# Where the slots of a mixture-of-experts layer go in a planned instruction stream: one chain, one piece a step, and the residual's store on another queue

## The chip, the cores and the metric

The kernel runs on one core of a Trainium2 chip. The metric is the device time of one execution in microseconds (us); the time of a kernel is the median of its runs. The engines are TensorE (PE in the profile; its weight loads are the row PEld), VectorE (DVE), ScalarE (ACT), GpSimd (POOL) and SyncE (SP, which only issues transfers here). Each of them works off its own list of instructions in order, and waits on semaphores for the others. Transfers between DRAM and the on-chip memory are issued by an engine's instruction and carried out by 16 DMA engines.

## The reference

The input is `x`, four sequences of 512 rows of 256 numbers, and a context of four times 1024 rows of 128. Two decoder layers follow each other, each made of residual blocks of the form `x = x + f(layernorm(x))`: a linear attention over landmarks, a causal attention that also reads the context (16 heads), a quantised linear layer; then a causal attention with hyperbolic distances, a block of two multi-head attentions with an MLP each (256 to 1024 to 256), and at last a mixture of experts. The change touches the order of work in the second block of the first layer and in the last two blocks of the second layer. The last one is:

```python
gate_scores = jax.nn.softmax(x @ Wg + bg, axis=-1)          # 8 experts
topk_scores, topk_idx = jax.lax.top_k(gate_scores, 2)
topk_scores = topk_scores / (jnp.sum(topk_scores, axis=-1, keepdims=True) + 1e-08)
combine_w = jnp.einsum('bsk,bske->bse', topk_scores, jax.nn.one_hot(topk_idx, 8))
for e in range(8):
    h = jax.nn.gelu(x @ W1[e] + b1[e])                      # 256 -> 1024
    y = h @ W2[e] + b2[e]                                   # 1024 -> 256
    output = output + y * combine_w[..., e:e + 1]
```

Here `x` is normalised; the block returns the unnormalised `x` plus `output`.

## The kernel before

**Slots.** The experts are not run on all rows. Each of the 2048 rows is copied (`scatter`, L1664: an indirect DMA, L1667, for 128 rows and one of their two choices, so eight for a batch) to its place in a table `rows` in DRAM, sorted by expert. The table is then worked off in `NSLOT` = 39 slots of 128 rows, each of one expert. For a slot the kernel fetches the rows (`fetch_z`, tile `zs`, 130 KB) and all weights of the slot's expert (`fetch_w`, tile `we`, 2052 KB, four buffers), both issued by SP (L1787 to L1807). Its work on the engines has three kinds of pieces. `turn` (L1809) transposes the rows on TensorE and makes on VectorE the row's target `to` (L1818) and its weight `wts` (L1820, L1821). `hidden` (L1823), in two halves, is the first layer: 16 matmuls (L1830) and 4 GELUs on ScalarE (L1832) a half. `output` (L1834) is the second layer, 16 matmuls (L1837, two for each of the program's eight calls), one multiplication on VectorE into `ys` (L1839) and one indirect DMA issued by POOL (L1840) that *adds* the 128 rows to the table `sums` in DRAM. `ys` has three buffers, `to` and `wts` four.

**What `sums` begins with.** Once a batch has passed the gate, `biases2` (L1683) puts the experts' second biases into `x`, and after its second half the batch's `x` is written to `sums` (L1688, L1689), issued by POOL. The slots' additions come on top of that. At the end `Slots.end` (L1876) copies `sums` to the output, two batches by SP and two by ScalarE.

**Early and late slots.** Which expert a slot belongs to depends on the data. After three of the four batches the first 16 slots (`NEARLY`) that are certainly full are known: `count_early` and `table_early` run as pieces of batch 2's gate, and `go` marks that the slots may begin. The other 23 are known after batch 3: `count_late` (L1771, whose `steps` issues 16 memsets on POOL, L1720) and `table_late` (L1776) are pieces of batch 3's gate, after `rank` (L1643) and ahead of `biases` (L1672, whose transposes are L1679), and `rest` (L1433 in the block's MLP) then adds their work.

**Who sets the order.** The program is written out by hand. `Stream` (L310 to L591) is a planner that runs while the program is built. A stream has *jobs*, here groups of four attention heads, and each job has first-pass tiles (`d_tile`, L381, scores and row maxima) and second-pass tiles (`a_tile`, L421, scores again, exponentials, values). A step `t` holds at most one first-pass tile (`d_at`) and one second-pass tile (`a_at`). All other work, such as norms, MLPs, gates, the slots, is cut into pieces and put into *chains*. A piece is a list of earliest step, due step, gap to the piece before, cost and function. A positive cost is time on TensorE, a negative one time on VectorE, zero is free. `chain` (L333) appends a chain. In each step `run` (L530) first lays the pieces that are due (`force`, L373), then the tiles, then calls `fill` (L357), which goes on laying the piece with the nearest due step while `room` (L369) allows it:

```python
return not cost or self.spent[k] == 0.0 or self.spent[k] + abs(cost) / 2 <= rates[k]
```

So the first piece of a step always goes, and further ones only up to the step's rate for TensorE (`rates[0]`) or VectorE (`rates[1]`). While there are first-pass tiles, the rate is worked out from the due steps; when there are none left it is fixed, 3.0 for both (L358). That is the case at the end of two streams: `l0_xattn` (the second block of layer 0) and `l1_xattn` (the double attention, whose end is also the gate and the slots).

**The slots in the planner.** When `go` has run and the attention is over, `tail` (L1293) closes the attention's pools and chains what `Slots.begin` (L1844) returns. It fetches rows of 16 slots and weights of three at once, and then, slot by slot (`round`, L1861): fetch of the slot after the next two (cost 0), two halves of `hidden` of the next slot (2.0 each), `turn` of the one after (0.5), `output` of this one (3.4). `rest` (L1433) makes a second chain of the rounds of the late slots. All these pieces have a due step far away, so they go behind the gate's pieces. `leave` (L1436) builds a batch's gate chain from the list that `gate` returns (L1691), and inserts the counting pieces by position from its end.

**The end of the other stream.** In `l0_xattn` each batch's preparation for the next attention (`front.batch`, 54 pieces, chained at L719 with `spill=True`) may be left over when the stream ends; its last pieces are given to `l1_attn` (L1014), whose `pump` (L1055) lays one at a time between its own units. That stage loads `qk` (L1069) from the DRAM tile `qk_d`, which these pieces fill (stores at L992), and multiplies it from L1092 on.

Of the kernel before, what the change touches and what calls it, by code (L numbers as in the profile page):

```python
# [20 lines left out]
P = 128  # L21
# [19 lines left out]
def decoder_kernel(ctx: ExitStack, tc: tile.TileContext, a: dict, out: bass.AP):  # L41
# [3 lines left out]
    def ts(i, n=P):  # L45
        return slice(i * n, (i + 1) * n)
# [263 lines left out]
    class Stream:  # L310
# [22 lines left out]
        def chain(self, items, spill=False):  # L333
            items = [[*i] for i in items]
            for i, j in zip(items[-2::-1], items[:0:-1]):
                i[1] = min(i[1], j[1])
            self.chains.append(SimpleNamespace(items=deque(items), at=-99, spill=spill))

        def lay(self, c):
            cost, fn = c.items.popleft()[3:]  # L340
# [14 lines left out]
            return rates  # L355

        def fill(self):  # L357
            rates = self.rates() if self.t in self.d_at else [3.0, 3.0]  # L358
            while True:
                ready = [  # L360
                    c for c in self.chains
                    if max(c.items[0][0], c.at + c.items[0][2]) <= self.t
                    and self.room(rates, c.items[0][3])
                ]
                if not ready:
                    return
                self.lay(min(ready, key=lambda c: c.items[0][1]))
# [871 lines left out]
    def l1_xattn(cn_d, moe, early):  # L1239
        with early.stack as st:  # L1240
# [52 lines left out]
            def tail():  # L1293
                if slots.ready:
                    inner.close()
                    s.chain([(s.t + 4, 10**6, 0, c, f) for c, f in slots.begin(st)])
                return slots.ready

            def block(k, b):
# [97 lines left out]
                def mlp():  # L1397
                    def li1(t):
                        ps = ring()
                        for g in range(4):  # L1400
                            PE.matmul(ps[:, 0:C], e.yT[:, g, ts(t)], w["li1"][:, g, :], start=g == 0, stop=g == 3)
                        add_to(e.xo[:, t, :], ps[:, 0:C])

                    def mid():
                        e.nT = one.tile([P, 2, T], F32, name="nT5", tag="nT5")
                        G.tensor_add(x1, x1, e.xo)
                        G.tensor_add(x1, x1, mid_bc(bl3, NT))

                    def li2(f):
                        if f == 0:  # L1410
                            e.h = one.tile([P, 8, T], F32, name="hT5", tag="hT5")
                        ps = ring()
                        for c in range(2):
                            PE.matmul(ps, w["li2"][:, c, ts(f)], e.nT[:, c, :], start=c == 0, stop=c == 1)
                        if f % 2:
                            S.activation(e.h[:, f, :], ps, AF.Identity, bias=pv[:, 12 + f : 13 + f])
                        else:
                            V.tensor_scalar_add(e.h[:, f, :], ps, pv[:, 12 + f : 13 + f])

                    def gelu():  # L1420
                        S.activation(e.h, e.h, AF.Gelu)
                        S.preload_act_table_set("natural_log_exp_and_others")
                        if k:
                            e.kept = one.tile([P, NT, C], F32, name="kept", tag="xo")
                            nc.sync.dma_start(e.kept, kept[b])

                    def li3(t):
                        ps = ring()
                        for f in range(8):
                            PE.matmul(ps[:, 0:C], e.h[:, f, ts(t)], w["li3"][:, f, :], start=f == 0, stop=f == 7)  # L1430
                        add_to(x1[:, t, :], ps[:, 0:C])

                    def rest():  # L1433
                        s.chain([(s.t, 10**6, 0, c, f) for c, f in slots.rest()])

                    def leave():  # L1436
                        if k:
                            G.tensor_add(x1, x1, e.kept)
                            g = gate(
                                moe, b, SimpleNamespace(), gs,  # L1440
                                lambda: one.tile([P, 2, T], F32, name="hT6", tag="hT6"), ring,
                            )
                            more = {
                                B - 2: [(1, 1.0, slots.count_early), (1, 1.0, slots.table_early)],
                                B - 1: [(1, 1.0, slots.count_late), (1, 1.0, slots.table_late)],
                            }.get(b, [])
                            g[-7:-7] = more
                            if more:
                                g[-3:-3] = [(0, 0.0, rest if b == B - 1 else slots.go)]
                            s.chain([(s.t, s.t + 2 + int(0.7 * i), gap, c, f) for i, (gap, c, f) in enumerate(g)])  # L1450
                        back.add(b)
                        if not k and b == B - 1:
                            ffn_weights("a2", ws[1])

                    t0 = s.t
                    work = [(True, 1.7, lambda: li1(0))] + [(False, 1.7, lambda t=t: li1(t)) for t in range(1, 4)]
                    work += [(1, -1.2, p) for p in ln_pieces(e.xo, z3)]
                    work += [(0, 0.0, mid), (True, 0.5, lambda: flip(e.z3, 0, [(e.nT, 8)]))]
                    work += [(False, 0.5, lambda: flip(e.z3, 1, [(e.nT, 8)]))]
                    work += [(f == 0, 1.7, lambda f=f: li2(f)) for f in range(8)]  # L1460
                    work += [(True, 0.0, gelu)]
                    work += [(t == 0, 3.4, lambda t=t: li3(t)) for t in range(4)]
                    work += [(False, 0.0, leave)]


                    lag, pace = {(0, 0): (1, 1.0), (0, B - 1): (3, 1.1), (1, B - 2): (2, 0.65)}.get((k, b), (3, 1.0))
                    s.chain([
                        (t0, t0 + (1 if i < 4 else lag + int(pace * (i - (i > 8)))), gap, c, f)
                        for i, (gap, c, f) in enumerate(work)
                    ])  # L1470
# [100 lines left out]
    def gate(m, b, e, gs, hT, bank):  # L1571
# [111 lines left out]
        def biases2(h):  # L1683
            ps = bank()
            for t in range(2):
                PE.matmul(ps[:, ts(t, C)], e.cT[:, ts(2 * h + t)], m.b2, start=True, stop=True)
            V.tensor_add(xb[:, ts(h, 2), :], ps.rearrange("p (t c) -> p t c", c=C), xb[:, ts(h, 2), :])
            if h:  # L1688
                G.dma_start(m.sums[ts(b, T), :].rearrange("(t p) c -> p t c", p=P), xb)  # L1689

        return (  # L1691
            [(2 if i == 0 else 1, -1.2, p) for i, p in enumerate(ln_pieces(xb, z))]
# [1 line left out]
            + [(1, -1.5, choose), (1, -1.2, choose2), (1, -1.2, choose3), (1, 0.5, rank)]  # L1694
            + [(t == 0, 0.0, lambda t=t: scatter(t)) for t in range(NT)]
            + [(1, 0.7, biases), (1, 0.9, lambda: biases2(0)), (0, 0.9, lambda: biases2(1))]
        )


# [312 lines left out]
```

## Time and profile before

| | us |
|---|---|
| median of 3 runs (lowest, highest) | 3477.65 (3476.08, 3499.53) |
| the profiled execution's own time | 3483.41 |
| its span | 3481.7 |
| TensorE, matmuls | 3066.6 busy, 88%, 19095 instructions |
| VectorE | 2092.8 busy, 60%, 5138 |
| ScalarE | 1902.4 busy, 55%, 3845 |
| GpSimd | 815.4 busy, 23%, 679 |
| granted TensorE clock, mean | 0.915 of full |
| DMA | 174.52 MB, mean 50 GB/s |

The span runs from the first to the last recorded instruction of one execution; the execution's own time is 1.7 us longer. Slices are 1/40 of the span, 87 us each. A group row gives the line, the engine and the operation, the tiles written and read, the number of instructions, then busy time and the mean of one, then the engine's idle time ahead of them and what ended most of it. In a row of windows each pair of brackets belongs to an engine (busy time and number of instructions, in the order TensorE matmuls, weight loads, VectorE, ScalarE, GpSimd), followed by the granted clock, the busy share of the DMA engines and GB/s. A timeline row has the start, the duration, the engine and the line; what stands in brackets at its end is the idle time before it and its releaser.

Three transfers matter here, with the median time from issue to landing: `we<-in_we`, 39 of 2052 KB, 9.1 us; `zs<-rows`, 39 of 130 KB, 8.8 us; `sums<-x`, four of 512 KB, 4.5 us.

### The profile page before, as it was taken

To read this page: it belongs to the slowest core of one execution; us is meant where nothing else is said; L and a number is where in the kernel's file an instruction comes from. 1 tells how busy PE (TensorE), PEld (TensorE's weight loads), DVE (VectorE), ACT (ScalarE), POOL (GpSimd) and SP (SyncE) were. 2 spreads that over 40 slices of the span, in tenths; PEclk is the share of its full clock that TensorE was granted. 3 is DMA by queue.
4 is the path that set the end of the run, shared out by engine and by line. 5 is a ranking of instruction groups with operands and counts; after the bars stand their busy time and mean duration, and the time that the engine had idled before them with its cause. 6 is when DMAs were issued, how large, how long until landed. Compare 5 with 4: busy or idle time off the path is not lost. (4 is left out here: it accounts for less than half of the span.)

```text
span 3481.7 us, 50606 instructions
## 1 busy us (share of the span) xinstructions
PE 3066.6 (88%) x19095; PEld 1497.5 (43%) x19095; DVE 2092.8 (60%) x5138; ACT 1902.4 (55%) x3845; POOL 815.4 (23%) x679
## 2 busy tenths in 40 slices
PE   6689999999998666677899999999999998987997
PEld 3433333334334344344434444433333333447896
DVE  4576676777765687876676565665746646433111
ACT  2225555454554764779588676556663664542221
POOL 1010112122022745668212121100101201122111
PEclk9889999999999567777799999999998999999998
DMA  9100000010001100120000000000000000045896
GB/s 287 55 28 7 1 7 3 6 31 4 10 19 42 49 6 32 37 86 7 25 1 1 1 4 16 7 1 31 13 1 5 21 1 13 13 172 172 288 310 190
DMA packets 78405, 174.52 MB, mean 50 GB/s; under 512 B 5640, under 2 KB 61200, under 8 KB 72976
## 3 DMA queue, kind: packets, MB, share of 16 engines
q1 hardware_dynamic: 68304, 155.47, 12.9%
q0 software_dynamic: 7728, 11.47, 1.5%
q10 hardware_dynamic: 2128, 4.34, 0.3%
q8 instruction: 150, 2.46, 0.3%
q14 instruction: 95, 0.78, 0.1%
HBM read 125.46 MB, written 47.90 MB: 50 GB/s over the span
## 5 line engine op out<-in xcount | busy, mean ns | idle before, releaser
L426 ACT ACTIVATE pt<-ps_s 128x512 f32<-128x512 f32 (+2 forms) x1536 | 792.1, 569 | 744.8 <-PE ps_s L425 649.6
L390 PE MATMUL ps_s<-kT,qT 32*128 32x512 f32 (+3 forms) x3072 | 923.0, 623 | 45.7 <-ACT pt L426 27.9
L402 DVE TENSOR_REDUCE mx<-ps_s 128x1 f32<-128x512 f32 x768 | 489.7, 684 | 221.7 <-PE ps_s L390 123.2
L390 PEld LDWEIGHTS ps_s<-kT,qT 32*128 32x128 f32 x3072 | 309.8, 186 | 338.8 <-issue 96.9
L394 DVE TENSOR_REDUCE mx<-ps_s 128x1 f32<-128x512 f32 x512 | 328.5, 685 | 193.4 <-PE ps_s L390 190.1
L425 PE MATMUL ps_s<-qa,kT 32*128 32x512 f32 (+3 forms) x1536 | 440.5, 588 | 4.5 <-ACT pt L426 3.1
L425 PE MATMUL ps_s<-qT,kT 32*128 32x512 f32 x1536 | 418.6, 638 | 0.0
L406 ACT ACTIVATE ps_s<-ps_s,mx 128x512 f32<-128x512 f32 x512 | 340.8, 670 | 27.5 <-DVE mx L394 27.0
L1832 ACT ACTIVATE hid<-ps_s,we 128x128 f32<-128x128 f32 x312 | 88.9, 368 | 236.4 <-issue 146.1
L1109 POOL TENSOR_TENSOR s<-s,mh 128x1280 f32<-128x1280 f32 x64 | 186.7, 2942 | 81.9 <-ACT mh L1108 64.1
L398 DVE CUSTOM_DVE_ANT_0 junk<-ps_s,dmask 128x256 f32<-128x256 f32 (+3 forms) x256 | 125.6, 491 | 92.0 <-PE ps_s L425 40.3
L1830 PE MATMUL ps_s<-zsT,we 128*128 128x128 f32 x1248 | 153.6, 283 | 26.6 <-DMA we<-in_we 14.8
L167 POOL TENSOR_TENSOR ln_r<-ln_ve,mhalf 128x4 f32<-128x4 f32 x40 | 40.8, 1020 | 532.5 <-DVE ln_ve L162 468.7
L1830 PEld LDWEIGHTS ps_s<-zsT,we 128*128 128x128 f32 x1248 | 150.9, 199 | 32.4 <-issue 17.1
L425 PEld LDWEIGHTS ps_s<-qa,kT 32*128 32x128 f32 x1536 | 143.3, 184 | 47.3 <-DVE mx L402 23.9
L1092 PE MATMUL ps_s<-qk 32*128 32x256 f32 (+3 forms) x512 | 103.2, 609 | 67.2 <-DVE mh L1097 56.5
L418 PE MATMUL ps_s<-qm,all 3*128 3x512 bf16 x768 | 156.9, 388 | 5.9 <-ACT ps_s L406 3.1
L1124 POOL TENSOR_TENSOR s<-s 128x1280 f32<-128x1280 f32 x64 | 147.6, 2337 | 12.3 <-ACT s L1120 12.3
L1151 DVE COPY pt<-ps_s 128x512 f32<-128x512 f32 x160 | 108.4, 688 | 62.0 <-PE ps_s L1149 62.0
L1149 PE MATMUL ps_s<-ident,s 128*128 128x128 f32 x640 | 130.5, 341 | 16.5 <-ACT s L1143 15.3
L1837 PE MATMUL ps_s<-we,hid 128*128 128x256 f32 x624 | 141.7, 381 | 0.0
L1097 DVE TENSOR_SCALAR_CACHE_REDUCE mh<-ps_s 128x512 f32<-128x512 f32 (+3 forms) x256 | 108.5, 487 | 51.7 <-PE ps_s L1096 27.4
(435 smaller groups left out, 5155.1 us busy)
## 6 DMA issues: line engine op xcount, KB each, us to landing
we<-in_we SPq DMA_DIRECT2D x39, 2052.0 KB, 9.1
rows<-zero SPq DMA_DIRECT2D x8, 2080.0 KB, 19.1
qk_d<-qkT SPq DMA_DIRECT2D x32, 256.0 KB, 2.5
qk<-qk_d SPq DMA_DIRECT2D x8, 1024.0 KB, 6.2
zs<-rows SPq DMA_DIRECT2D x39, 130.0 KB, 8.8
li<-in_a_li SPq DMA_DIRECT2D x4, 1024.0 KB, 5.5
v_d<-vp SPq DMA_DIRECT2D x16, 143.5 KB, 1.8
v<-v_d SPq DMA_DIRECT2D x4, 574.0 KB, 6.8
```

The costliest lines, as they stand in the source:

```text
L390: PE.matmul(ps[:, 0:n], u.qT[r, ts(qt)], u.kT[r, hf * 512 : hf * 512 + n], start=True, stop=True)
L394: V.tensor_reduce(m, ps[:, 0:n], AX.X, ALU.max, negate=True)
L402: V.tensor_reduce(m, ps[:, 0:n], AX.X, ALU.max)
L406: S.activation(ps, ps, AF.Exp, bias=m, accum_out=sm)
L418: PE.matmul(ps, self.ones[r, :], u.qm[r, :], start=True, stop=False)
L425: PE.matmul(ps[:, c0:], u.kT[r, ts(kt)], (u.qa if u.first_row else u.qT)[r, c0:], start=u.first_row, stop=True)
L426: S.activation(u.pt[:, j, c0:], ps[:, c0:], AF.Exp, scale=u.scale)
L1109: G.tensor_add(s, s, m)
L1124: G.tensor_mul(s, s, s)
L1149: PE.transpose(ps[:, ts(j)], u.s[h // 2][:, h % 2, c0 : c0 + P], ident)
L1830: PE.matmul(ps[:, ts(f)], u.w[:, k : k + P], u.zT[:, c, :], start=c == 0, stop=c == 1)
L1837: PE.matmul(ps[:, 0:C], u.h[:, f, :], u.w[:, 2048 + f * C : 2048 + f * C + C], start=f == 0, stop=f == 7)
```

## The change

There are four edits.

1. `fill` uses a TensorE rate of 1.0 instead of 3.0 in steps that have no first-pass tile. With `room` as above, a step then gets one TensorE piece beside pieces of cost zero, unless a second one is cheap enough (0.5 after 0.5 or 0.7). VectorE's rate stays 3.0.
2. `tail` keeps the early slots' chain in `slots.chain`, and `rest` appends the late slots' pieces to it (and lists the chain again if it has run empty) instead of making a chain of their own.
3. The store of a batch's `x` into `sums` is no longer part of `biases2(1)` and no longer issued by POOL; it is a piece of its own, the gate's last one, a step later or more, of cost zero, issued by ScalarE.
4. Since the gate's list is one longer, the two positions at which the counting pieces and `go` or `rest` are inserted move by one, so that they stay at the same places.

```diff
             self.chains.append(SimpleNamespace(items=deque(items), at=-99, spill=spill))
+            return self.chains[-1]
...
         def fill(self):
-            rates = self.rates() if self.t in self.d_at else [3.0, 3.0]
+
+            rates = self.rates() if self.t in self.d_at else [1.0, 3.0]
...
                     inner.close()
-                    s.chain([(s.t + 4, 10**6, 0, c, f) for c, f in slots.begin(st)])
+                    slots.chain = s.chain([(s.t + 4, 10**6, 0, c, f) for c, f in slots.begin(st)])
...
                     def rest():
-                        s.chain([(s.t, 10**6, 0, c, f) for c, f in slots.rest()])
+                        c = slots.chain
+                        if not c.items:
+                            s.chains.append(c)
+                        c.items.extend([s.t, 10**6, 0, cost, f] for cost, f in slots.rest())
...
-                            g[-7:-7] = more
+                            g[-8:-8] = more
                             if more:
-                                g[-3:-3] = [(0, 0.0, rest if b == B - 1 else slots.go)]
+                                g[-4:-4] = [(0, 0.0, rest if b == B - 1 else slots.go)]
...
             V.tensor_add(xb[:, ts(h, 2), :], ps.rearrange("p (t c) -> p t c", c=C), xb[:, ts(h, 2), :])
-            if h:
-                G.dma_start(m.sums[ts(b, T), :].rearrange("(t p) c -> p t c", p=P), xb)
+
+        def store():
+            nc.scalar.dma_start(m.sums[ts(b, T), :].rearrange("(t p) c -> p t c", p=P), xb)
...
             + [(1, 0.7, biases), (1, 0.9, lambda: biases2(0)), (0, 0.9, lambda: biases2(1))]
+            + [(1, 0.0, store)]
```

## The prediction

> **What bounds the kernel now.** I read the page's slices first: TensorE is busy nearly throughout, but in the last ten slices the DMA row climbs from 0 to 9 while VectorE, ScalarE and GpSimd fall to 1. So the end is a stage of its own, the mixture-of-experts slots. Then the chain that ended last:
>
> ```profile
> DMA sums<-ys,to 5%; DVE wts L1821 0%; DVE to L1818 0%; DVE wts L1820 0%; POOLq L2008 0%; DVE ys L1839 0%; POOLq L1840 0%
> ```
>
> Five per cent of the span is one thing: the accumulating scatter of each slot's output (L1840). Next, the instructions of the tile `sums`:
>
> ```profile
> L1840 POOL DMA_INDIRECT sums<-ys,to x39: 1536/1543/1659, 3110.4 to 3468.3; - x39
>   DMA sums<-x: 12.5, 1
> DMA to landing us min/median/max: 3.5/6.5/12.6
> ```
>
> There are 39 adds, and each waits for the one before it to land: in the timeline an add is issued about 0.7 us after its forerunner landed (issued 3256.51, landed 3264.30, next issued 3265.02). The add of slot 6 is issued at 3227.36 and that of slot 38 at 3468.34, so 32 steps took 240.98 us, 7.53 each: 201.8 for the 25 steps up to slot 31 (8.07 each), 39.2 for the last 7. After the last add come 13.4 us (landing, the copy to the output, the end).
>
> By stage (busy times, then clock, DMA share, GB/s):
>
> ```profile
> 3095.00:3200.00 105.00, 89.75 (x521) 75.05 (x520) 38.88 (x152) 33.66 (x77) 22.61 (x32) 0.95 0.59 209
> 3200.00:3230.00 30.00, 19.04 (x114) 17.58 (x113) 2.85 (x11) 5.40 (x20) 6.94 (x6) 0.83 0.55 199
> 3230.00:3380.00 150.00, 146.20 (x1004) 136.73 (x1002) 22.90 (x95) 45.62 (x160) 29.33 (x19) 1.00 0.93 311
> 3380.00:3440.00 60.00, 50.46 (x313) 46.65 (x313) 8.25 (x35) 13.69 (x48) 10.80 (x7) 0.91 0.75 244
> ```
>
> From 3230 to 3380 three limits lie close together: TensorE's slot period is 7.24 us (rows below), the DMA engines are 0.93 full, and the adds come at 7.57. The adds are the slowest, so their lag on TensorE grows by 0.3 us a slot. From 3371 to 3429 the lead is used up: TensorE waits for VectorE, which stands at L1818 until an add has landed, and six steps take 9.65 each.
>
> **The change, part by part.** The built program of the changed kernel shows its order. No instruction is added; four POOL transfers become ScalarE ones; everything else is a move.
>
> *1. One TensorE piece a step.* Until the last batch's gate is done TensorE now gets, as slot work, `hidden` of slots 0, 1 and 2, four `turn`s and one `output`; before, `hidden` of slots 0 to 6 and six `output`s. What the old filling cost the chain that leads to the late table:
>
> ```profile
> 3188.41 1.01 PE L1679 MATMUL ps_s<-ident,gp 128*8 128x128 f32 x4 [9.25 <-DVE gp L1676]
> 3189.64 4.33 PE L1837 MATMUL ps_s<-we,hid 128*128 128x256 f32 x16
> 3203.17 3.73 PE L1830 MATMUL ps_s<-zsT,we 128*128 128x128 f32 x32
> 3206.74 0.38 PE L1812 MATMUL ps_s<-ident,zs 128*128 128x128 f32 x2
> 3206.96 3.62 PE L1837 MATMUL ps_s<-we,hid 128*128 128x256 f32 x16
> 3221.54 5.56 PE L1830 MATMUL ps_s<-zsT,we 128*128 128x128 f32 x32 [10.96 <-DMA we<-in_we]
> ```
>
> An output is 3.62 us, half a hidden 1.95; one slot starts every 7.24. Removed from the path: ahead of the MLP's second layer an output and half a hidden, 5.6, with the gaps between them 6 (L1414 starts at 3112.1, now about 3106); ahead of the gate's transposes and scores 1.5 + 1.8; between `choose` and `choose3` one turn and one `ys` on VectorE, 1.4; ahead of `rank` 1.6. Sum 12.3. Added: the turn of slot 2 between the halves of the gate's norm, 0.9. So `rank`, whose indices stood at 3173.2, ends near 3162.
>
> [...] The trace: after 10.96 us of idling the first `hidden` takes 5.56 instead of 3.73, 1.8 more, at a granted clock of 0.83 for that window. [...] Part of it is paid today too (L1430 starts after 3.7 idle), so I take 3, and `rank` ends at 3165.
>
> *2. POOL's queue.* Before, six adds sit on POOL among the gate's work, and the memsets of `count_late` (L1720) wait behind the fifth until 3180.8:
>
> ```profile
> DVE more L1713 <- POOL full L1720: 6.0, 1, 6.0
> ```
>
> Now one add precedes them, so they run early and the eight scatters (L1667) start at 3165 instead of 3182.7. They go at 2.73 each, 20.1 in all: POOL is free at about 3185. The biases follow `rank` by 23.0 now (3173.7 to 3196.6); without 8.3 of turn, `ys` and memset wait and 5 of output and turn it is 9.7: 3175.
>
> *3. The store by ScalarE.* Queued behind the two are:
>
> ```profile
> 3207.72 0.97 POOL L1667 DMA_INDIRECT rows<-gz,idx  x1 [1.77 <-DMA rows<-gz,idx]
> 3214.01 0.84 POOL L1689 DMA_DIRECT2D sums<-x  x1 [3.41 <-DVE wts L1821]
> 3227.36 1.60 POOL L1840 DMA_INDIRECT sums<-ys,to  x1 [12.51 <-DMA sums<-x]
> ```
>
> Before, POOL stores at 3214 and the next add waits 12.5. Now ScalarE issues it at 3176, past POOL's scatters; waiting with it on ScalarE are only slot 3's GELUs, whose matmuls end later. It may seem that the 12.5 vanish. [...] At 3176 few weights are in flight; I take 3182, hidden under the scatters. The three earlier stores cost ScalarE 0.7 each (its L1878 issues take 0.60 to 0.79) where TensorE bounds (88.4 of the 90 us from 2950 to 3040): nothing, at worst 2. POOL loses waits of up to 18.8, which nobody waited for.
>
> *4. Late slots in the early chain.* Before, the fetch of slot 16 stood on SP ahead of the weights of slots 9 and later, and waited for the scatters until 3210: that is the 10.96 wait for weights. Now it stands in its place after slot 15's. That wait is gone, but it lay where the adds were late anyway.
>
> *The sum of the end.* The add of slot 1 starts when scatters and store are done: 3185 to 3188, taken 3187. From there 37 steps remain, where before 32 remained at 3227. The changed kernel starts its series 40 us earlier with five more adds, and five adds at 8.07 are 40. With 8.07 to slot 31: 30 x 8.07 + 39.2 = 281. With TensorE's lead kept longer (27 steps of 7.57, 3 of 9.65, 39.2): 273. Between: 277. End 3187 + 277 + 13.4 = 3477.4 against 3481.7: **-4.3**.
>
> *5. The end of the first attention.* The same rate also holds after its last first-pass tiles. Three pieces of batch 2 (two `turn`s, a `lift`) move into the next stage's pump, and the last batch's 54 pieces start three pumps later.
>
> ```profile
> 1116.45 10.60 SPq L992 DMA_DIRECT2D qk_d<-qkT  x8
> 1135.79 2.09 PE L1092 MATMUL ps_s<-qk 32*128 32x512 f32 x8 [9.09 <-DMA qk<-qk_d]
> ```
>
> The load that TensorE awaits for 9.1 us stands behind eight stores, now four: it comes about 6 earlier. Paid back: in the pumped stage ten units take 375 us where ten quiet ones take 260, so 115 / 54 = 2.1 a piece, three pieces 6. Net 0; bounds -6 (pieces hidden) and +12 (they fall where units already take 57 and 59).
>
> Total -4.3. The profiled execution took 3483.41, 1.7 more than its span and 5.8 more than the median; I carry the difference to the median: 3477.65 - 4.3 = **3473**.
>
> **Rivals.**
> *Faster.* If VectorE's wait at L1818 never closes, TensorE's 7.24 sets the pace: 33 x 7.24 + 4 x 4.83 (the last four steps now) = 258, end 3458.6, and with -6 from part 5: 3449. For it: TensorE is never short of weights now. Against: the adds needed 7.57 even while TensorE ran evenly.
> *Slower, one mechanism.* The 9.65 state comes early. It is entered when an add's issue lags its output by about 14.5 us (reached now at slot 25). The new start has a lag of about 7; should the first steps take over 8, the lead is gone by slot 11, and 20 steps at 9.65, 10 at 7.57 and 39.2 make 308: end 3508, time 3504. For it: six steps in a row did so. Against: it began only after 17 even slots.
> *No effect.* Starts and numbers of adds cancel (-40, +40), as above, so that 3478 is within reach of the first case.
>
> **How the numbers follow.** Likeliest 0.62, own range 3458 to 3490 (step price 7.6 to 8.2: 33 x 0.3 = 10 each way; part 5). Faster 0.18; slower 0.20. The range takes in both: 3444 to 3506. One per cent, 35 us, is about what a measurement of this kernel can tell from no change. Faster by that (under 3443) needs the faster case and more: 0.09. Slower by that (over 3512) needs the slower case and part 5's bad end: 0.10. Same 0.81.
>
> **What would show it.** First scatter near 3165, POOL free near 3185, slot 1's add near 3187, 37 steps of about 7.5, no 11 us wait for weights, first L1092 about 6 us earlier, the pumped stage no shorter. I am wrong if slot 1's add comes after 3195, if the steps' mean leaves 7.2 to 7.9, or if the stage between 1136 and 1650 changes by over 12.

## The result, and the profile after

The changed kernel takes 3516.41 us (median of 8 runs, 3502.5 to 3530.91) against 3476.95 for the kernel before (8 runs, 3470.03 to 3499.53). The ratio is 1.0105, with a 95% interval from 1.0074 to 1.0136: 26 to 47 us slower, some 36. The forecast was 3473, in a range of 3444 to 3506.

The profiled execution of after is the longest of its eight, 3530.91 with a span of 3529.2, so that the two profiles differ by 47.5 us where the medians differ by 39. Its time is followed from landmark to landmark (us; lines of before, then of after):

| | before | after | difference |
|---|---|---|---|
| first product of `qk` (L1092, L1094) | 1135.8 | 1133.1 | -2.7 |
| first MLP product of the last block (L1414, L1416) | 1914.6 | 1950.0 | +35.4 |
| last batch: last product of the MLP (L1430, L1432) | 3147.1 | 3182.9 | +35.8 |
| last batch: first scatter (L1667, L1673) | 3182.7 | 3206.1 | +23.4 |
| add of slot 6 (L1840, L1848) | 3227.4 | 3271.6 | +44.2 |
| add of slot 38 | 3468.3 | 3515.7 | +47.4 |
| span | 3481.7 | 3529.2 | +47.5 |

So 35 of 47 us are lost before the slots begin, in the stage that my fifth part had at zero, and 12 in the end, where I had a gain of 4. First the stage that was lost: the products of `qk`, before and after, in the view of that line (durations least, median, most in ns, then the first and last start).

```profile
L1092 PE MATMUL ps_s<-qk x512: 270/577/1218, 1135.8 to 1630.6; 32*128 32x128 f32 x43, 32*128 32x384 f32 x43, 32*128 32x256 f32 x43, 32*128 32x512 f32 x42
...
  DMA qk<-qk_d: 9.1, 1
```

```profile
L1094 PE MATMUL ps_s<-qk x512: 269/586/1218, 1133.1 to 1666.2; 32*128 32x128 f32 x43, 32*128 32x384 f32 x43, 32*128 32x256 f32 x43, 32*128 32x512 f32 x42
...
  DMA qk<-qk_d: 6.8, 1
```

The first one starts 2.7 us earlier, having waited 6.8 for its load instead of 9.1, as forecast in kind. The last one starts 35.6 later.

Then the end. The adds and the store in the view of `sums`, and GpSimd's timeline with the scatters of the last batch:

```profile
L1848 POOL DMA_INDIRECT sums<-ys,to x39: 1540/1552/1656, 3193.7 to 3515.7; - x39
L1696 ACTq DMA_DIRECT2D sums<-x x4: 366/374/395, 2755.5 to 3220.5; - x4
...
DMA to landing us min/median/max: 2.9/6.7/11.2
```

```profile
3206.09 1.02 POOL L1673 DMA_INDIRECT rows<-gz,idx  x1 [10.04 <-DVE gp L1662]
3209.37 0.97 POOL L1673 DMA_INDIRECT rows<-gz,idx  x1 [2.27 <-DVE endL L1736]
...
3220.34 0.97 POOL L1673 DMA_INDIRECT rows<-gz,idx  x1 [1.72 <-DMA rows<-gz,idx]
3224.82 0.97 POOL L1673 DMA_INDIRECT rows<-gz,idx  x1 [3.51 <-DMA rows<-gz,idx]
3233.54 0.97 POOL L1673 DMA_INDIRECT rows<-gz,idx  x1 [7.75 <-DMA rows<-gz,idx]
3234.81 1.61 POOL L1848 DMA_INDIRECT sums<-ys,to  x1 [0.30 <-issue]
3242.97 1.56 POOL L1848 DMA_INDIRECT sums<-ys,to  x1 [6.55 <-DVE wts L1829]
```

The memsets no longer hold up the scatters and the store no longer holds back an add (it is issued at 3220.5, the add of slot 1 waits 0.30 behind the last scatter). But the eight scatters take 27.4 us from first to last instead of 25.0, since two of them wait 3.5 and 7.8 for the one before. From there the adds go as forecast: 37 steps in 280.9 us, 7.59 each.

By stage, with the prediction's four windows moved by the 35.4 us that were lost before, so that they hold about the same work:

```profile
3130.40:3235.40 105.00, 81.39 (x377) 63.83 (x376) 37.71 (x137) 26.58 (x51) 19.80 (x32) 0.84 0.42 151
3235.40:3265.40 30.00, 30.00 (x209) 28.31 (x209) 5.29 (x21) 9.68 (x35) 6.60 (x5) 1.00 0.95 318
3265.40:3415.40 150.00, 144.97 (x973) 135.95 (x972) 22.74 (x96) 43.90 (x155) 30.06 (x20) 0.98 0.90 304
3415.40:3475.40 60.00, 52.47 (x344) 48.07 (x342) 7.64 (x34) 15.97 (x56) 9.30 (x6) 0.97 0.83 278
```

In the first window, up to the last scatter, TensorE does less (81.4 us, 89.8 before) at a granted clock of 0.84 instead of 0.95. In the second it now works throughout (30.0 us instead of 19.0): the wait for weights is gone. The last two are much as before.

### The profile page after: what moved, and what is told of

Read it like the earlier page. It is cut to its first block, busy times and chain, and to the rows that moved or that the text cites. A ratio compares the mean times of both kernels' runs of the same rounds, so it can differ in the third digit from the quotient of the medians.

```text
span 3529.2 us, 50592 instructions
## 1 busy us (share of the span) xinstructions
PE 3095.2 (88%) x19095; PEld 1514.7 (43%) x19095; DVE 2122.9 (60%) x5138; ACT 1903.2 (54%) x3845; POOL 812.4 (23%) x675
## 4 chain that ended last, share of the span: by engine, by line
PE 61%; DVE 14%; DMA 10%; issue 7%; ACT 6%; POOL 2%; SPq 0%; POOLq 0%; ACTq 0%; DVEq 0%
PE ps_s L392 16%; DMA sums<-ys,to 7%; PE ps_g L523 7%; PE ps_s L427 4%; PE ps_s L667 3%; PE ps_s L1416 3%; PE ps_s L1362 3%; PE ps_s L1432 3%; PE ps_s L420 2%; PE ps_s L1151 2%; PE ps_s L1403 2%; PE ps_g L530 2%; DMA rows<-gz,idx 2%; PE ps_s L1094 2%; PE ps_s L1373 1%
## 5 line engine op out<-in xcount | busy, mean ns | idle before, releaser
L1840 ACT ACTIVATE hid<-ps_s,we 128x128 f32<-128x128 f32 x312 | 88.8, 368 | 236.1 <-issue 173.9
L1094 PE MATMUL ps_s<-qk 32*128 32x256 f32 (+3 forms) x512 | 111.2, 674 | 66.6 <-DVE mh L1099 53.5
```

The lines of the kernel that those rows point to most:

```text
L1094: PE.matmul(ps[:, 0:n], qk[rr, 0, gg, ts(qt)], qk[rr, 1, gg, 0:n], start=True, stop=False)
```

## The experiments

All times are given as ratios to the kernel before on the same chip, with 95% intervals; one per cent is 35 us. "The stretch" is the time from the first product of `qk` to the first MLP product of the last block, 778.8 us before and 816.9 after.

### Which edit costs what

The rate is one number for two streams. Two kernels split it. The first is the changed kernel with

```diff
-            rates = self.rates() if self.t in self.d_at else [1.0, 3.0]
+            rates = self.rates() if self.t in self.d_at else [1.0 if self.last else 3.0, 3.0]
```

where `self.last` is true for `l1_xattn` alone; the second is the kernel before with the opposite choice, `[3.0 if self.last else 1.0, 3.0]`.

> The changed kernel with the TensorE rate of 1.0 kept for the last stream only; the stream of layer 0 has 3.0 again. Theory A (the loss of the changed kernel lies in the pumped stage, where its MLP inputs come 35.4 us late): the stretch from the first qk product to the first L1414-type matmul falls back from 816.9 to about 779 us, and what is left is the tail, +12 us: about 3477 + 12 = 3489. Theory B (the loss lies in the tail and the later arrival is noise of one profile): the time stays near 3516.

Measured: 1.0039 (1.0026 to 1.0052); stretch 774.3.

> The kernel before with only the rate of the first stream's end at 1.0; tail, chains and store as before. Theory A: the first qk product comes about 3 us earlier, the stretch from there to the first L1414 matmul grows from 778.8 to about 817, time about 3477 + 35 = 3512. Theory B: 3477.

Measured: 1.0123 (1.0083 to 1.0163); stretch 810.2. So the loss is made in both places: 13.6 us are left when the first stream is let alone, and that stream's rate alone costs 29 to 57. The two mid values add up to 56, more than the 36 of the whole; their lower ends, 29 and 9, add up to 38, inside its interval of 26 to 47. The last MLP product comes 35.8 us late in the profile of after, 25.6 in that of this second kernel, though both have the same pumped stage: a stretch read from one profile is good to some 7 us.

The other edits of the end, one by one and together. The kernel before with the rate of 1.0 in the last stream only:

> The kernel before with only the rate of 1.0 in the last stream; late slots in a chain of their own, store by GpSimd. Theory rate: +13 us or more, 3492, with matmuls of the gate (scores, biases) near twice as long as before. Theory store: about 0, 3479.

Measured: 1.0053 (1.0038 to 1.0068). The kernel before with the store alone (its own piece, issued by ScalarE):

> The kernel before with only the store as a piece of its own, issued by ScalarE. My prediction's estimate: the 12.5 us that the next add waited are hidden behind the scatters, but the adds are paced by one another, so that up to 12 us could come out of the end: -12 to 0. Theory store of the tail's loss: +5 to +13 (the store's 512 KB run while the last scatters do, and hold them back).

Measured: 1.0011 (0.9993 to 1.0028). The changed kernel with the rate back at `[3.0, 3.0]`, which leaves one chain and the store:

> The changed kernel with the TensorE rate of 3.0 everywhere: of the change only the one chain for early and late slots and the store by ScalarE are left. The kernel with the rate of 1.0 in the last stream alone (one chain, store, no loss in the pumped stage) stood 0.39% above the kernel before, +13.6 us. Theory rate (the tail loses because TensorE, with one piece a step, idles ahead of the gate and works at a lower clock, and because late slots have five more adds to go): this kernel falls back to the kernel before, 3479 within 5, or some us below since the store's landing of 12.5 us no longer holds back an add and the 11 us wait for weights is gone. Theory store (the store in the scatters' way, or the chain, costs it): this kernel stays near +13.

Measured: 0.9984 (0.9964 to 1.0004). One quantity orders these kernels, the time from the last MLP product to the add of slot 6, read from each one's profile:

| slot 6's add, us after the last MLP product | rate 3.0 | rate 1.0 in the last stream |
|---|---|---|
| two chains, store by GpSimd | 80.3 (before) | 95.2 (1.0053) |
| two chains, store by ScalarE | 80.7 (1.0011) | |
| one chain, store by ScalarE | 73.1 (0.9984) | 88.3 (1.0039), 88.7 (after) |

The rate costs 15 us in either row, the single chain saves 7 in either column, the store moves nothing. The 32 steps after slot 6 took from 228 to 250 us in these profiles, without an order that goes with the edits, so that the order of the times by slot 6 is one of six profiles and not a proof.

### The pumped stage

The change moves three left-over pieces into the pump and lets the last batch's 54 pieces start three pumps later. Empty pieces do the second without the first:

```diff
             for c in left:
                 c.at = -99
+            left[-1].items.extendleft([[0, 0, 1, 0.0, lambda: None]] * 3)
```

> The kernel before with three empty pieces ahead of the 54 pieces of the last batch that are pumped between the attention units: no work is added, every piece falls three pumps later. Theory place (what costs is where in a unit a piece falls, above all the ScalarE pieces of the gate for spikes and roots, which then stand ahead of a unit's logarithms): the stretch grows by 20 to 32 of the 35 us, time 3497 to 3509. Theory number (what costs is the work of the three left-over pieces themselves, and the stores that they issue): no more than one further unit at some 36 instead of 26, +10, time near 3480 to 3487.

Measured: 1.0092 (1.0063 to 1.0122); stretch 803.5, 24.7 more than before.

> As with three empty pieces, but five: a whole unit has five pumps, so that every piece falls at the same place of a unit as before, one unit later. Theory place: the stretch grows by 0 to 12 us (one unit more that is not quiet), time 3477 to 3489, clearly less than with three. Theory number, or a cost of being late as such: no less than with three empty pieces.

Measured: 1.0021 (0.9998 to 1.0045); stretch 783.7. No work was added in either. Three pumps late cost 25 us, five cost 5. It is the place in a unit that counts. The unit times show the rest: a quiet unit takes 26.0; above that, the pumped units take 115 us in sum before, 139 with three empty pieces, 117 with five, and 151 after. So of the changed kernel's 35 us, 24 are the place and 12, by difference, the three pieces. These sums repeat within 5 us: the units of before stand unchanged in two kernels above, `[3.0, 3.0]` and the first of the two that split the rate, and take 111 there; the second of those has the units of after and takes 151.

What is it about the place? My first guess was ScalarE. In the kernel before it stands 11.6 us for VectorE ahead of one exponential (L952), with a unit's own exponentials behind it. A gap of three pumps puts that piece behind the next unit's square roots:

```diff
-            work += [(apart, 0.0, power), (1, -2.0, cosh)]
+            work += [(3 * apart, 0.0, power), (1, -2.0, cosh)]
```

> The kernel before with a gap of 3 pumps instead of 1 ahead of the last batch's exponential (the piece called power), so that it is laid after the next unit's square roots and no longer among a unit's exponentials, where ScalarE stood 11.6 us for VectorE. Theory place in its sharper form (the price of a pumped piece on ScalarE is the time until VectorE, behind in its own list, has made its input): the wait goes, the unit of 56.8 us becomes some 45, and the pieces after it fall two pumps later, which may give back a few us: -12 to -4, about 3470. If the place is only a matter of chance with no such rule: anything between -10 and +25.

Measured: 1.0031 (1.0015 to 1.0048), slower. The wait is gone, and the unit still takes 56.1 us instead of 56.8: the wait was slack, and the pieces behind it, two pumps later, spoilt another unit (37.2 instead of 26.0). That guess fell.

The windows of single units say who fills them. Three rows, in the prediction's columns: the longest unit of before, a quiet one of before, and the longest with three empty pieces.

```profile
1313.41:1370.24 56.83, 36.73 (x212) 21.35 (x212) 37.50 (x95) 26.29 (x34) 42.03 (x22) 0.73 0.05 18
...
1523.92:1549.88 25.96, 22.95 (x198) 13.08 (x197) 18.94 (x65) 25.74 (x33) 19.21 (x10) 0.86 0.13 42
```

```profile
1369.03:1430.09 61.06, 38.66 (x240) 21.80 (x243) 50.93 (x110) 26.65 (x36) 32.27 (x16) 0.74 0.17 54
```

ScalarE fills a quiet unit (25.74 of 25.96). In the long ones it does no more than that; the busiest is GpSimd in the first (42.0 of 56.8) and VectorE in the second (50.9 of 61.1). Over the stretch VectorE is busy 23.7 us longer with three empty pieces, for the same 1347 instructions (before, then with them):

```profile
1135.80:1914.60 778.80, 594.12 (x4192) 316.40 (x4192) 560.52 (x1347) 587.64 (x966) 403.63 (x220) 0.78 0.08 26
1138.00:1941.50 803.50, 595.07 (x4193) 316.60 (x4193) 584.25 (x1347) 587.82 (x966) 403.78 (x220) 0.78 0.07 25
```

Where these come from stands in the timelines of VectorE and GpSimd of the kernel with three empty pieces, and in the same VectorE line where GpSimd's work is left out (the next experiment; busy time, then the mean in ns):

```profile
1421.18 2.29 DVE L947 TENSOR_TENSOR n<-n,n 128x128 f32<-128x128 f32 x1
1423.51 2.81 DVE L948 TENSOR_SCALAR n<-n 128x128 f32<-128x128 f32 x1
1426.35 0.95 DVE L949 RECIPROCAL n<-n 128x128 f32<-128x128 f32 x1
```

```profile
1418.68 4.65 POOL L1125 TENSOR_TENSOR s<-s 128x1280 f32<-128x1280 f32 x2
1423.29 5.81 POOL L1110 TENSOR_TENSOR s<-s,mh 128x1280 f32<-128x1280 f32 x2
```

```profile
L948 DVE TENSOR_SCALAR n<-n 128x128 f32<-128x128 f32 x1 | 0.2, 227 | 0.0
```

GpSimd's first addition runs from 1423.29 to about 1426.2. VectorE's L948, 0.23 us by itself, starts just behind it and takes 2.81, until 1426.32. It is no single case: in this stage VectorE's operations on 128 x 4 numbers take 0.2 us and, where they meet GpSimd's of 2.3 to 2.9, mostly 1.5 to 2.8. That VectorE stands there until GpSimd's instruction ends is my reading of these rows. To weigh it, the units' work on GpSimd is left out (additions of the roots, squares; distances are others then), without and with three empty pieces:

```diff
-                    G.tensor_add(s, s, m)
...
-                for s in u.s:
-                    G.tensor_mul(s, s, s)
```

> The kernel before without GpSimd's additions and multiplications in the pumped stage's units (the sum of the two square roots, the squares, and the same for the minima are left out; output and distances are therefore others). Theory contention (an instruction of VectorE that meets one of GpSimd takes until that ends: 4-element operations of 0.2 us took 1.8 to 2.8 in the pumped units): VectorE's busy time in the stage falls from some 400 us by 25 to 60 for the same instructions, and the pumped units shrink; the quiet units stay at 26.0, since ScalarE fills them. Rival (VectorE's time is that of its own work, the place of a piece counts through ScalarE's waits): VectorE's busy time as before within 5, units as before but for a few us.

Measured: 0.9753 (0.9733 to 0.9773), stretch 685.7: 93 us less. VectorE's busy time in it falls from 560.5 to 478.4 us for the same 1347 instructions, more than the 60 that I had as the most. The pumped units take 28 us above 26.0 in sum, where they took 115. Waits for GpSimd's results are gone too, so that not all of the 93 need be contention.

> The same without GpSimd's work in the units, with three empty pieces ahead of the last batch's 54. With GpSimd's work the three empty pieces cost 24.7 us of the stretch to the first L1414 (803.5 against 778.8) and VectorE was busy 25.4 us longer in it. Theory contention: without GpSimd's work the two kernels differ by less than 8 us there, and VectorE's busy times by less than 5. Rival (bunching of pieces, or ScalarE's waits): the difference stays near 20 to 25.

Measured: 0.9765 (0.9744 to 0.9786), stretch 700.8. VectorE's busy time in the stretch now differs by 1 us between the two (478.4 and 479.4), as expected. The stretch still differs by 15.1 in these profiles, where I expected less than 8, and the times by 6.

With nearly half of GpSimd's work in ten units moved instead of left out, the first ten units' squares on ScalarE:

```diff
                 for s in u.s:
                     S.activation(s, s, AF.Ln, scale=1024.0)
+                if u.n < 10:
+                    for s in u.s:
+                        S.activation(s, s, AF.Square)
```

> The kernel before with the squares of the first ten units on ScalarE. Theory contention: 25 to 35 us less, 3447; rival: up to 50 more.

Measured: 0.9931 (0.9910 to 0.9951); stretch 748.4.

> The same with three empty pieces ahead of the last batch's. With GpSimd's full work three empty pieces cost 27.7 us of the time (24.7 of the stretch), without it 6 (15 of the stretch in its profile). Theory contention: 12 to 20 us above the same kernel without them. Rival (the loss is bunching alone): 25 and more.

Measured: 0.9962 (0.9943 to 0.9982); stretch 761.7, 13.3 more.

> The changed kernel as it is, with the squares of the first ten units on ScalarE. Theory contention: the loss of its pumped stage (35 us: 24 of place, 11 of three more pieces) shrinks to some 22, and it stands 20 to 30 above the same edit on the kernel before (of which 13 in the tail); its time near 3475. Rival: 35 or more above it.

Measured: 1.0037 (1.0019 to 1.0054); stretch 772.3, 23.9 more than the same edit on the kernel before. The loss of the stretch thus shrank from 38 to 24. By time the kernel stands 31 us (medians) to 37 us (ratios) above the one with the same edit, where I expected 20 to 30 and the rival 35 or more; the tail's 13 are in that. The times do not show that the loss shrank.

Three empty pieces thus cost 24.7 us of stretch with all of GpSimd's work, 13.3 with about half and 15.1 with none; in the sum of the units alone 23, 19 and 14; in the median time of the whole kernel 28, 11 and 6. So some of the loss goes with GpSimd's work and some stays without it: by the two traces about 10 and 15 of the 25, by the times more of it is contention. The share is not settled. The longest unit of the kernel without GpSimd's work and with three empty pieces shows what stays:

```profile
1323.43:1371.81 48.38, 38.64 (x257) 22.29 (x256) 37.75 (x125) 26.64 (x37) 0.00 (x0) 0.77 0.22 69
```

TensorE works 38.6 and VectorE 37.8 of 48.4 us: three of the four `tokens` pieces and the norm and roots that follow them have fallen into one unit. Without the empty pieces all four lay in one, of 38.2, and what follows in the next, of 37.3. That they wait for each other there is read from the trace, and no run takes it apart further.

### The end

Does the clock carry part of the 15 us? These are TensorE's rows around the gate's scores, before and after, then with nine products of the identity (result unused) at the end of each light step of the last stream, to fill the idle time. That kernel has the first stream's rate back at 3.0.

```profile
3158.00 1.04 PE L1593 MATMUL ps_s<-ident,gz 128*128 128x128 f32 x8
...
3160.66 1.85 PE L1600 MATMUL ps_s<-wg,hT 128*128 128x8 f32 x16
```

```profile
3191.34 0.65 PE L1599 MATMUL ps_s<-ident,gz 128*128 128x128 f32 x2 [2.55 <-DVE gz L195]
3192.70 1.65 PE L1599 MATMUL ps_s<-ident,gz 128*128 128x128 f32 x6 [0.71 <-DVE gz L195]
3194.28 3.90 PE L1606 MATMUL ps_s<-wg,hT 128*128 128x8 f32 x16
...
3215.94 3.75 PE L1692 MATMUL ps_s<-b,hT 8*128 8x256 f32 x8 [0.86 <-DVE hT L1687]
```

```profile
3157.77 2.17 PE L596 MATMUL ps_s<-ident 128*128 128x128 f32 x18
3159.78 1.85 PE L1611 MATMUL ps_s<-wg,hT 128*128 128x8 f32 x16
```

> The changed kernel with the first stream's rate back at 3.0 (the kernel that stands at 1.0039 of before, +13.6), and in the tail nine matmuls of the identity (some 2.1 us, result unused) on TensorE at the end of each step that has no long TensorE piece, so that it doesn't idle for 4 to 7 us ahead of the MLP's transposes, the gate's scores and the biases. Theory clock (the gate's matmuls took twice their time, 3.90 against 1.85 for the scores, 2.29 against 1.04 for the transposes, 3.75 against 1.99 for the biases, because TensorE had idled before): they are back at the short times, the first scatter comes 4 to 6 us earlier, slot 6's add too, and the time falls to about 1.0025 of before. Rival (the times are long for another reason, or the path does not run through TensorE): no change, or later by the two us of each filling.

Measured: 1.0000 (0.9984 to 1.0017), all 13.6 us back, three times what I expected. The granted clock from 3147 to 3177 is 1.00, where after had 0.78 from 3182.5 to 3212.5, and the scores take 1.85 again and not 3.90. But the first scatter hardly comes earlier (3168.8; without filling 3169.0): the fillings cost about what they save. What comes earlier is the end of the scatters:

```profile
3168.80 1.02 POOL L1678 DMA_INDIRECT rows<-gz,idx  x1 [8.60 <-DVE gp L1667]
...
3186.26 0.97 POOL L1678 DMA_INDIRECT rows<-gz,idx  x1 [1.86 <-DMA rows<-gz,idx]
3189.56 0.97 POOL L1678 DMA_INDIRECT rows<-gz,idx  x1 [2.33 <-DMA rows<-gz,idx]
3190.83 1.61 POOL L1853 DMA_INDIRECT sums<-ys,to  x1 [0.30 <-issue]
```

They take 20.8 us instead of 27.2, and the add of slot 6 comes 80.4 us after the last MLP product instead of 88.3. What had held the seventh scatter up goes with the load of a slot's weights, in the view of its line for the 35 us around the scatters, first after, then with filling:

```profile
L1805 SPq DMA_DIRECT2D we<-in_we x3: 337/338/338, 3225.1 to 3239.5; - x3
```

```profile
L1810 SPq DMA_DIRECT2D we<-in_we x2: 337/337/337, 3189.2 to 3196.4; - x2
```

After, it is issued at 3225.1, 0.3 us behind the seventh scatter, which then needs 8.0 us to land. With the fillings TensorE's slot work is later (its `output` ends at 3189.1, without filling at 3187.9), so the buffer comes free later: the load goes at 3189.2, when the seventh scatter has landed. So the clock is back in this kernel, and the gain came by another route than I had. That the loads do it shows in all 19 traces of this case: each of the 28 last-batch scatters that took more than 4.5 us to land had a weight load in flight with it. In before it is the scatter at 3194.42, 0.3 us behind a load.

Are the adds the bound of the end at all? With slots adding in turns to two tables (the second one is not added to the output):

```diff
-                self.m.sums, bass.IndirectOffsetOnAxis(ap=u.to, axis=0), y, None, compute_op=ALU.add
+                self.m.sums2 if u.s % 2 else self.m.sums, bass.IndirectOffsetOnAxis(ap=u.to, axis=0), y, None, compute_op=ALU.add
```

> The kernel before with the slots' additions going in turns to two tables, so that each waits for the add before the last one (the second table is not added to the output, and is set to zero at the start, 2.2 MB of stores more). If the chain of adds paces the end, as the prediction has it, then 32 steps from slot 6 fall from 241 to about 32 x 7.24 = 232 or what the weights allow, VectorE's waits at the target's conversion are gone, and the end comes 5 to 20 us earlier: 3460 to 3475. If TensorE or the weights pace it and the adds only trail: no change, 3479.

Measured: 0.9955 (0.9936 to 0.9974). GpSimd waits for `ys`, TensorE's result, and no longer for an add, and the steps are even:

```profile
3338.98 1.54 POOL L1842 DMA_INDIRECT sums<-ys,to  x1 [5.70 <-DVE ys L1841]
3346.22 1.54 POOL L1842 DMA_INDIRECT sumz<-ys,to  x1 [5.70 <-DVE ys L1841]
3353.47 1.54 POOL L1842 DMA_INDIRECT sums<-ys,to  x1 [5.70 <-DVE ys L1841]
```

7.24 a step: this is TensorE's slot period, and the adds' chain had been the bound. Its price is again that of company: in the 19 traces the 108 adds with no weight load in flight until they had landed took 3.5 to 4.5 us to land, those beside two loads mostly in 6 to 9, and the last steps of before, when all weights are there, are 4.4 apart. Then the scatters should go between the adds. Two at a time, in the last batch, on one chain and rate 3.0 (the gate's last nine pieces also have later due steps, so that they are not forced together):

```diff
-            + [(t == 0, 0.0, lambda t=t: scatter(t)) for t in range(NT)]
+            + [(2 if b == B - 1 else t == 0, 0.0, lambda t=t: scatter(t)) for t in range(NT)]
```

> One chain for early and late slots, rate 3.0, the store by ScalarE (the kernel at 0.9984 of before), and in the last batch two of the eight scatters at a time between two adds on GpSimd, instead of all eight in a row. A scatter waits 1.7 us for the one before it and an add some 6 for its forerunner, so that a pair fits into an add's wait: the block of 26 to 31 us, in which no add goes, is gone, and slot 6's add comes some 20 earlier after the last L1430 (73 before). If adds pace the end: 3476 - 20 = 3456, 0.994 of before. If TensorE or the weights pace it: 3470 or more.

Measured: 0.9987 (0.9970 to 1.0004): nothing. Slot 6's add did come earlier, 50.2 us after the last MLP product instead of 73.1, but the 32 steps after it took 255 us instead of 234. Three adds went between the scatters, at the price of longer scatters. GpSimd's timeline, and SP's weight loads in the stretch:

```profile
3189.24 1.58 POOL L1852 DMA_INDIRECT sums<-ys,to  x1 [7.13 <-DVE ys L1851]
3191.13 1.01 POOL L1677 DMA_INDIRECT rows<-gz,idx  x1 [0.31 <-issue]
3193.95 1.00 POOL L1677 DMA_INDIRECT rows<-gz,idx  x1 [1.81 <-DMA rows<-gz,idx]
...
3208.55 1.60 POOL L1852 DMA_INDIRECT sums<-ys,to  x1 [0.30 <-issue]
3214.76 0.98 POOL L1677 DMA_INDIRECT rows<-gz,idx  x1 [4.60 <-DMA rows<-gz,idx]
3222.58 0.96 POOL L1677 DMA_INDIRECT rows<-gz,idx  x1 [6.84 <-DMA rows<-gz,idx]
3223.84 1.59 POOL L1852 DMA_INDIRECT sums<-ys,to  x1 [0.30 <-issue]
```

```profile
L1809 SPq DMA_DIRECT2D we<-in_we x5: 337/338/338, 3197.5 to 3229.0; - x5
```

The first pair waits 1.8 us in between, though an add went 1.9 us ahead of it; the later ones wait 4 to 7, and a pair and an add then take 10 to 15. What is new there is a weight load every 7 to 9 us. So that expectation was wrong by the landing time of a scatter beside a weight load; that an add in flight holds a scatter up does not show.

### A version that beats both

One chain, the store by ScalarE, rate 3.0, and the squares of ten units on ScalarE:

> One chain for early and late slots, rate 3.0, store by ScalarE (0.9984 of before), and in the first ten of the sixteen units of the pumped stage the squares are made by ScalarE instead of GpSimd: four operations of some 1.25 us a unit there, 9.4 of GpSimd's 21 us a unit gone. Theory contention: without any of GpSimd's work the pumped units' excess over 26 us fell from 115 to 32 in sum; with 45% of it gone it falls by some 37, units never below 31, a quiet unit or two pay 5: 25 to 35 us less, near 3445. Rival (a unit is bound by ScalarE, its work adds up): ten times 5 more, 3520.

Measured: 0.9924 (0.9906 to 0.9941), 3450.04 us against 3476.14: 26 us faster than before and some 63 faster than the change. Nearly all of that is the squares': by themselves they gave 0.9931.

## Why the prediction was wrong

**Part 1, TensorE's order: failed in its size.** `rank` was to end near 3165; in after it does at 3206.2, which is 3170.8 when the 35.4 us of the earlier stage are taken off. The 6 us ahead of the MLP's second layer were 1.3 (its first product starts at 3146.2, or 3110.8): what filled TensorE there had been hidden behind the norm on VectorE, for which it now waits 4.2 us. No run shows the 3 that I took for the clock. What after shows in its place is some 6, at a granted clock of 0.84 in this stage where before had 0.95: the MLP's two layers are 0.9 and 0.8 longer, its transposes and the gate's 1.3 each and the scores 2.0.

**Part 2, POOL's queue: half right.** The memsets run early and VectorE's wait for them is gone. The scatters' 20.1 was the wrong number: I took 2.73 each, as if none met a transfer. In before they had taken 25.0, with one of 7.7 beside a weight load, and after they took 27.4, with one of 4.5 beside the store and one of 8.7 beside weight loads.

**Part 3, the store: right.** It is issued 9 us later than I put it (3185 when shifted), hidden behind the scatters, and by itself it changes nothing (1.0011). The landing at 3182 no run shows: in after the store landed 3.7 us after its issue (3188.8 when shifted), in before 12.6.

**Part 4, the late slots: right, and undervalued.** The wait for weights is gone. I gave it no price, since the adds were late anyway; the single chain saves 7 us, with either rate.

**The sum of the end.** Its form held: a start for slot 1 and then steps of a known price. Steps: 277 forecast, 280.9 measured. Start: 3187 forecast, 3199.4 measured (3234.8 shifted). That start is 12 of the 16 us between -4.3 and +12, the steps are 4. It is also one of the signs of being wrong that I had named (after 3195).

**Part 5, the first attention's end: this step failed.** "115 / 54 = 2.1 a piece, three pieces 6", with 12 as the worst case of the whole step. The three pieces cost 12, twice what I took. What is missing altogether is the price of moving the other 54, which I had as "start three pumps later" and at nothing, with no reason given: 24 us. An average price per piece says nothing of where the pieces fall, and the view that would have shown it was at hand. Before, the pumped units took from 29 to 57 us for five pumps each; I used only their sum. With the 25 to 35 us that this step measured, the forecast would have been 3498 to 3508, and with the end's 16 it would have been 3514 to 3524, with the measured 3516 among them.

The rival on the slower side put its loss in an early series of adds at 9.65 a step; such steps came only late, seven of them, where before had six. That the rate's second place would decide was in no rival.

What stays open: why runs of steps of 9 to 11 us come at changing places (slots 15, 16 and 27 to 32 in after, 26 to 30 in before); how the two parts of the place, contention and bunching, share the changed kernel's own 24 us.

## What to carry to other kernels

A planner's parameter acts wherever its code runs: look for every place, and where it moves a block of work against another engine's rhythm, price the block and not only what was added. Ask of each moved instruction what it meets at its new place, on its own engine and on the others; here a gain of 21 us lay there (four operations a unit moved to ScalarE in ten units, 0.9984 to 0.9924), in a stage that the change was not about. And a filler that is taken off a busy engine frees time only on the path that really waits for that engine.

## What the runs showed of the hardware

- A 0.2 us instruction of VectorE took up to 2.9 us where it met one of GpSimd (L962 with three empty pieces, 2.92, and 0.22 without GpSimd's work); taking GpSimd's 21 us of each 26 away shortened VectorE's 1347 instructions of one stage from 560.5 to 478.4 us and the stage by 93 us of 779. VectorE instructions that read PSUM at the same time (L1098 of the kernel with three empty pieces, 128 x 512, 0.63 to 0.69 us) were not stretched: in before they took 0.69 with GpSimd at work and 0.69 without.
- An indirect scatter landed in 2.5 us alone, in 4.2 beside a 512 KB store (after, 3220.3; two others beside an earlier store, at 3118.4 and 3121.3, in 2.6 and 2.4) and in 8.0 beside a 2 MB weight load. An accumulating one landed in 3.5 to 4.5 us with no such load in flight, and mostly in 6 to 9 beside two.
- In after the granted clock was 0.71 from 3185.5 to 3202, where TensorE had idled 2.6 and 0.7 us with 0.65 us of work between; the scores took 3.90 us instead of 1.85. With products of the identity in the gaps it was 1.00 (3147 to 3177), and the scores took 1.85.
